# Turning token rows for routing and experts: from TensorE transposes to transposing DMAs, with the tile numbers dealt anew

## The chip, the cores and the metric

The kernel runs on one core of one Trainium2 chip, in float32. The metric is the device time of one execution in microseconds. Instructions run on five engines: TensorE (PE, matrix products and transposes; its weight loads are listed as PEld), VectorE (DVE), ScalarE (ACT), GpSimd (POOL) and SyncE (SP, which here only issues DMAs). A DMA can be issued from the queue of SP, ACT or POOL (in the profile SPq, ACTq, POOLq). Each engine works its own instructions in order and waits where one of them needs something that isn't there yet.

## What is computed

`x` has 3327 rows of 256 numbers, `adj` is a 0/1 matrix of 3327 x 3327. Two layers follow each other:

```python
x = x + gat0(layernorm(x), adj)       # 2 heads of 128; softmax over the neighbours
x = x + moe(layernorm(x))             # 16 experts, 2 for each token
x = x + gat1(layernorm(x), adj)       # 1 head of 256, elu
x = x + recurrent_ffn(layernorm(x))   # 30 steps

# moe
logits = h @ gate_w + gate_b
top_probs, top_idx = top_k(softmax(logits), 2); top_probs /= sum(top_probs)
y = sum over the two experts e of top_prob * ((silu(h @ w1[e]) * (h @ w2[e])) @ w3[e])
```

Here `w1` and `w2` of an expert are 256 x 512 and `w3` is 512 x 256, 1.5 MB together. The change touches only the mixture of experts (`moe`) and what leads up to it.

## The kernel before

**Tiles.** The tokens are padded to 3328 = 26 tiles of 128 (`NP`, `NT`). The span has these stages: first projection (to 53 us), first attention (53 to 388), experts (388 to 752, with the wait for the results' landing at its end), second projection (to 788), second attention (to 1088), recurrence (to 1839).

**First attention (`attend`).** Destination rows are taken in five groups `groups0` of 4, 6, 6, 6 and 4 tiles, each for two heads: ten parts. In each part a loop over `j` runs through the 26 source tiles: ACT makes `e` (L276), DVE masks it to `pT` (L281), PE adds up one product for each destination tile (L286; 1352 products of two passes each in this attention, counted from its start). Between the steps, from `j = 2` on, one piece of other work is let in: first the pieces of `closing` (division by the softmax sum and the residual, then, after the second head, the routing of the rows that are now final: the generator `route`), then those of `later` (the token lists, and the search for the tiles). One `yield` in `route` is thus one step of `j` later in the program. The adjacency comes group by group: GpSimd brings bytes into `in_bytes` (L325), SP turns them into `adjT` by transposing DMAs (L335), one for each tile, 425 KB each. What a group needs is asked for when the lists of an earlier group have been issued. `put_factors` and `row_factors` (L227, L234) spread the row factors, partly over SP.

**Routing (`route`, for one group).** The rows are normalized into `row` (`normalized`: DVE statistics, a power on GpSimd at L121, DVE at L128), stored as float32 in the table `table_x` in DRAM (L516, ACT's queue), and turned on PE two tiles at a time (`turned`, L148; ACT copies the result out of PSUM, L149). The turned rows are the stationary side of the gate products (L526). DVE then finds the two best experts and each token's place in that expert's list, and GpSimd writes token number and weight into `lists` with an indirect DMA for each tile and choice (L592). Group 4 is routed during the first expert tiles, by `aside`.

**Tiles of experts.** `find_tiles` cuts the lists into tiles of 128 tokens of one expert each: 16 from the full tiles of the first three groups (`FIRST`), 45 more when all are routed (61 are `ALWAYS` worked off; further ones only if the data want them). For tile number `s` it gives the expert (`table[0]`), whether its matrices differ from those of tile `s - 3` (`table[1]`), the tokens (`which`), the places of the results (`to`) and the weights. There are `SETS` = 3 sets of matrices; tile `s` uses set `s % 3`, and `weights(s)` loads 1.5 MB on SP (L800 to L802) only where `table[1]` is set.

**Working off (`work_off`).** For tile `s`: GpSimd gathers 128 rows of `table_x` (`gathered`, L761, four tiles ahead), PE turns them by two transposes (`features_first`, L826), ACT copies them to `hT` (L827), PE makes two products of 16 passes each (`product`, L835), ACT the silu (L881), DVE the product of both (L885), PE `results` of the tile before (8 passes, L851), DVE its weighting (L854) and GpSimd scatters it into `given` (L855). In PE's queue a tile is: products of `s`, transposes of `s + 1`, results of `s - 1`.

**Order.** The instruction order within each engine is set by the tile framework's scheduler from this program order, with priorities; the pools (`bufs`) decide what may run ahead. The recurrence already turns its rows by 16-bit planes: ACT parts each float32 into its two 16-bit halves (L1095), SP writes them to DRAM (L1097) and a transposing DMA brings them back with tokens along the free axis (L1107), so that two halves lie beside each other as one float32 again.

Of the kernel before, what the change touches and what calls it, by code (L numbers as in the profile page):

```python
# [31 lines left out]
def gat_moe_gat_recurrent_ffn(ctx: ExitStack, tc: tile.TileContext, a: dict, out: bass.AP):  # L32
# [315 lines left out]
    table_x = dram.tile([NP, D], F32, name="table_x")  # L348
# [33 lines left out]
    with ExitStack() as moe:  # L382
# [125 lines left out]
        turn = moe.enter_context(tc.tile_pool(name="turn", bufs=2))  # L508

        def route(ts):  # L510
# [3 lines left out]
            normalized([x[:, t, :] for t in ts], [row[:, j, :] for j in range(n)])  # L514
            here = slice(t0 * P, (t0 + n) * P)
            nc.scalar.dma_start(table_x[here, :].rearrange("(t p) d -> p t d", p=P), row[:, :n, :])  # L516
            yield

            if ts is not groups0[-1]:
                yield  # L520
            pg = bank()[:, : n * E].rearrange("p (j e) -> p j e", e=E)
            for j0 in range(0, n, 2):
                hT = turned(row[:, j0 : j0 + 2, :], turn, ps)
                for j in range(2):
                    for k in range(KD):
                        nc.tensor.matmul(  # L526
                            pg[:, j0 + j, :], lhsT=hT[:, j, k, :], rhs=gw[:, k, :], start=(k == 0), stop=(k == KD - 1)
                        )
                yield
# [81 lines left out]
            if ts is groups0[3]:  # L611

                for s in range(3):
                    ahead.append(gathered(s))
# [36 lines left out]
        numbers(two[:, 0, :], [[1, SLOTS]], 0, 0)  # L651
# [10 lines left out]
        def find_tiles(end, s0, n):  # L662
# [30 lines left out]
            tile_no = two[:, 0, :n]  # L693
# [61 lines left out]
        places = []  # L755

        def gathered(s):
            if s % 3 == 0 or s == ALWAYS:
                places.append(rows_p.tile([P, MOST * P], F32, name="rb"))
            row = places[-1][:, (s % 3) * D : (s % 3 + 1) * D]  # L760
            nc.gpsimd.indirect_dma_start(  # L761
                out=row, out_offset=None, in_=table_x[: EARLY * P, :] if s < FIRST else table_x,
                in_offset=bass.IndirectOffsetOnAxis(ap=which[:, s : s + 1], axis=0),
            )
            return row
# [56 lines left out]
        def features_first(row):  # L822
            pt = ps_o.tile([P, 512], F32, name="acc0")[:, :D].rearrange("p (k q) -> p k q", k=KD)
            hT = turn.tile([P, 2, KD, P], F32, name="hT")[:, 0]
            for k in range(KD):
                nc.tensor.transpose(pt[:, k, :], row[:, k * P : (k + 1) * P], ident)  # L826
            nc.scalar.copy(hT, pt)  # L827
            return hT

# [13 lines left out]

        ahead = deque()
# [16 lines left out]
        def work_off(s0, s1, aside):  # L861

            hT = features_first(ahead.popleft())
            made = None
            for s in range(s0, s1 + 1):
# [10 lines left out]
                if s < s1:  # L876
                    if s + 4 < s1:
                        ahead.append(gathered(s + 4))
                    pa = product(hT, ew[s % SETS][0])
                    act = edge("e")  # L880
                    nc.scalar.activation(act, pa, AF.Silu)  # L881
                    next(aside, None)
                    pb = product(hT, ew[s % SETS][1])
                    made = edge("pT")
                    nc.vector.tensor_tensor(made, act, pb, ALU.mult)  # L885
                    if s + 1 < s1:
                        hT = features_first(ahead.popleft())
                if s > max(s0, 1):
                    results(s - 1, hidT)
                if s + SETS - 1 < s1:  # L890
# [14 lines left out]
        ahead.append(gathered(3))  # L905
        weights(1)

# [26 lines left out]
        with tc.If(more > ALWAYS - FIRST):  # L934
            ahead.extend(gathered(s) for s in range(ALWAYS, ALWAYS + 4))
            for s in range(ALWAYS, ALWAYS + SETS - 1):
                weights(s)
# [275 lines left out]
```

## Time and profile before

| | us |
|---|---|
| median of the runs | 1838.48 |
| lowest and highest of 3 runs | 1833.5, 1839.01 |
| the profiled execution | 1841.14 |
| its span, first to last instruction | 1839.4 |
| PE busy in the span | 1787.4 |
| DVE, ACT, POOL busy | 1319.1, 1223.9, 888.4 |
| mean granted TensorE clock | 0.995 of full speed |
| expert transposes L826 | 122 of 273 ns |
| routing transposes L148 | 52 of 283 ns |
| their copies out of PSUM, L149 and L827 | 586 and 372 ns each |
| gather L761, mean | 979 ns of POOL, 61 times |
| list entry L592, mean | 1222 ns of POOL, 52 times |

A line of a timeline has the start in microseconds, the length, the engine (a "q" behind it marks a DMA issue: its length is that of the issue, not of the transfer), the source line, the operation, what is written from what, and how many instructions were joined; in square brackets, the idle time of the engine before it and what ended that. A line of groups has the count, then busy time in all, the mean in nanoseconds, and the idle time before. Windows list the busy time of each engine in a stretch, then the granted TensorE clock as a share of full speed, the mean busy share of the 16 DMA engines and what they moved in GB/s. Matmuls are pipelined, so their durations overlap: starts are the better measure.

### The profile page before, as it was taken

Reading aid. Unit: us, or ns where it says so; the run is one execution under the profiler, and the core shown is the slowest. Engines: PE = TensorE matmul, PEld = TensorE weight load, DVE = VectorE, ACT = ScalarE, POOL = GpSimd, SP = SyncE. Lnnn points to the kernel's source line nnn. Section 1 sums busy time; section 2 is a strip of 40 time slices with the busy share of each in tenths; the row PEclk is TensorE's granted clock in tenths of the full one; section 3 lists DMA queues with packets and bytes.
Section 4 is the critical chain, followed back from the end, with each engine's and each line's share of the span. In section 5 each row is a group of like instructions: output and inputs, shape, how many; then the busy total and the mean of one; then the engine's idle time right before and its main releaser. Section 6 shows DMA issues by size and latency. Waiting matters only on the chain.

```text
span 1839.4 us, 32502 instructions
## 1 busy us (share of the span) xinstructions
PE 1787.4 (97%) x10980; PEld 1631.7 (89%) x10980; DVE 1319.1 (72%) x4039; ACT 1223.9 (67%) x1587; POOL 888.4 (48%) x654
## 2 busy tenths in 40 slices
PE   7999999999999999799999999999999999999997
PEld 6999999898999999688888878888888888888886
DVE  6888878853222222657677678999999999999998
ACT  2877667642111111366666579999999999999994
POOL 3010212155333332100111028988898889888984
PEclk9999999999999999899999999999999999999999
DMA  8887360258999886400000036666667666666667
GB/s 178 114 123 91 66 101 16 67 187 255 349 345 333 304 301 225 159 9 22 14 18 22 12 84 172 172 172 168 171 167 178 173 172 172 172 167 169 175 172 218
DMA packets 458610, 284.44 MB, mean 155 GB/s; under 512 B 305269, under 2 KB 418220, under 8 KB 458442
## 3 DMA queue, kind: packets, MB, share of 16 engines
q1 hardware_dynamic: 442322, 249.47, 48.4%
q0 software_dynamic: 11440, 28.09, 8.8%
q10 hardware_dynamic: 4680, 4.76, 0.8%
q8 instruction: 90, 1.47, 0.3%
q14 instruction: 78, 0.64, 0.1%
HBM read 168.19 MB, written 91.69 MB: 141 GB/s over the span
## 4 chain that ended last, share of the span: by engine, by line
PE 67%; issue 10%; DVE 6%; POOL 5%; DMA 3%; ACT 1%; another core or an unknown queue 0%; SPq 0%; POOLq 0%; DVEq 0%; ACTq 0%
PE po L1120 35%; PE acc L286 24%; PE bank L1085 4%; DVE pT L281 3%; POOL given L855 2%; POOL rb L761 2%; DMA given<-wh,to 2%; PE bank L835 1%; PE acc L163 1%; PE bank L148 1%; DMA old<-kept 1%; PE bank L526 1%; PE acc L851 1%; DMA lists<-pair,ati 0%; DVE x L1130 0%
## 5 line engine op out<-in xcount | busy, mean ns | idle before, releaser
L276 ACT ACTIVATE e<-rb,minus,full 128x384 f32<-128x384 f32 (+3 forms) x494 | 399.2, 823 | 168.6 <-DVE pT L281 150.8
L1055 POOL TENSOR_TENSOR th<-th,x 128x1024 f32<-128x1024 f32 (+1 forms) x210 | 465.0, 2214 | 94.1 <-ACT th L1052 86.4
L281 DVE SCALAR_TENSOR_TENSOR pT<-e,part,adjT 128x384 f32<-128x384 f32 (+3 forms) x494 | 383.5, 782 | 117.8 <-PE acc L286 101.9
L1120 PE MATMUL po<-wc,adjT 128*128 128x256 f32 x1888 | 422.2, 379 | 0.0
L1120 PEld LDWEIGHTS po<-wc,adjT 128*128 128x128 f32 x1888 | 356.4, 190 | 47.6 <-DVE x L1130 0.3
L1130 DVE SCALAR_TENSOR_TENSOR x<-po,rr,bb 128x256 f32<-128x256 f32 x780 | 325.1, 478 | 61.8 <-PE po L1120 61.2
L286 PE MATMUL acc<-wh,pT 128*128 128x129 f32 x2704 | 311.0, 276 | 2.3 <-DVE pT L281 2.3
L286 PEld LDWEIGHTS acc<-wh,pT 128*128 128x128 f32 x2704 | 305.5, 192 | 3.6 <-DVE pT L281 3.0
L286 PE MATMUL acc<-s_wh,pT 128*128 128x257 f32 x1352 | 295.5, 381 | 3.6 <-DVE pT L281 3.6
L286 PEld LDWEIGHTS acc<-s_wh,pT 128*128 128x128 f32 x1352 | 255.8, 190 | 42.7 <-DVE pT L281 7.0
L1120 PE MATMUL po<-wc,zT 128*128 128x256 f32 x1232 | 281.0, 379 | 0.8 <-DVE x L1130 0.8
L1064 DVE BATCH_NORM_STATS2 stats<-z 128x6 f32<-128x256 f32 x780 | 274.1, 412 | 1.4 <-ACT z L1059 1.4
L1120 PEld LDWEIGHTS po<-wc,zT 128*128 128x128 f32 x1232 | 229.2, 190 | 29.7 <-issue 1.1
L1095 ACT COPY adjT<-z 128x1024 int16<-128x1024 int16 x236 | 235.2, 1044 | 4.8 <-DVE pT L281 2.0
L121 POOL TENSOR_TENSOR rstd<-ve,neg_half 128x4 f32<-128x4 f32 (+3 forms) x28 | 32.0, 1141 | 410.4 <-DVE ve L119 312.3
L1052 ACT ACTIVATE th<-x 128x1024 f32<-128x1024 f32 (+1 forms) x210 | 209.2, 996 | 29.0 <-DVE x L1130 23.8
L1075 POOL TENSOR_TENSOR rr<-rr,neg_half 128x4 f32<-128x4 f32 (+1 forms) x210 | 206.8, 985 | 26.4 <-DVE rr L1070 26.3
L1059 ACT ACTIVATE z<-th 128x1024 f32<-128x1024 f32 (+1 forms) x210 | 207.0, 986 | 7.9 <-POOL th L1055 1.8
L885 DVE TENSOR_TENSOR pT<-e,bank 128x512 f32<-128x512 f32 x61 | 41.9, 688 | 179.7 <-PE bank L835 119.6
L881 ACT ACTIVATE e<-bank 128x512 f32<-128x512 f32 x61 | 36.4, 597 | 196.9 <-PE bank L835 117.2
L835 PEld LDWEIGHTS bank<-hT,wh 128*128 128x128 f32 x1280 | 149.6, 192 | 9.3 <-issue 4.5
L835 PE MATMUL bank<-hT,wh 128*128 128x128 f32 x1280 | 150.6, 276 | 6.5 <-ACT hT L827 2.5
(196 smaller groups left out, 1546.6 us busy)
## 6 DMA issues: line engine op xcount, KB each, us to landing
wh<-in_w_dram SPq DMA_DIRECT2D x120, 512.0 KB
apart<-adjT SPq DMA_DIRECT2D x236, 256.0 KB
first_set<-in_w_dram SPq DMA_DIRECT2D x63, 512.0 KB
in_bytes<-in_adj_dram POOLq DMA_DIRECT2D x3, 2496.0 KB
adjT<-apart SPq DMA_TRANSPOSE x236
x<-in_x_dram SPq DMA_DIRECT2D x6, 512.0 KB
kept<-x SPq DMA_DIRECT2D x8, 384.0 KB
old<-kept SPq DMA_DIRECT2D x6, 512.0 KB
```

The costliest lines, as they stand in the source:

```text
L276: nc.scalar.activation(e[:, : n * P], rb[:, : n * P], AF.Relu, scale=sc.full[:, j, h : h + 1], bias=sc.minus[:, j, h : h + 1],)
L281: masked = nc.vector.scalar_tensor_tensor(pT[:, : n * P], e[:, : n * P], sc.part[:, j, h : h + 1], adjT[:, j // 2, ts[0] * P : (ts[-1] + 1 ...
L286: nc.tensor.matmul(po[c], lhsT=pT[:, c * P : (c + 1) * P], rhs=wh[:, j, h, :], start=(j == 0 and c % per_bank == 0), stop=(j == NT - 1), s ...
L835: nc.tensor.matmul(p[:, f, :], lhsT=w[:, k, f * P : (f + 1) * P], rhs=hT[:, k, :], start=(k == 0), stop=(k == KD - 1),)
L1052: self.put(nc.scalar.activation(self.th, self.hs, AF.Tanh, scale=1.0 / S))
L1055: self.put(nc.gpsimd.tensor_tensor(self.th, self.th, self.hs, ALU.add))
L1059: self.put(nc.scalar.activation(self.z, self.th, AF.Silu, scale=1.0 / S))
L1064: self.put(nc.vector.bn_stats(stats[:, j, :], self.z[:, j, :]))
L1075: self.put(nc.gpsimd.tensor_tensor(r, r, neg_half[:, : self.n], ALU.pow))
L1095: self.put(nc.scalar.copy(parts[:, c : c + 2], halves[:, c : c + 2]))
L1120: nc.tensor.matmul(self.po[:, j, :], lhsT=self.zT(j, k), rhs=wc[:, k, :], start=(k == 0), stop=(k == KD - 1),)
L1130: nc.vector.scalar_tensor_tensor(self.hs[:, j, :], self.po[:, j, :], self.r[:, j : j + 1], bb, op0=ALU.mult, op1=ALU.add)
```

## The change

Three things are changed together.

1. `table_x` holds each row as two planes of 16-bit halves (`[NP, 2 * D]` of int16; the same bytes as before, parted). `route` parts the normalized rows with ACT copies, two tiles at a time into one buffer `planes`, writes each pair from ACT's queue, and then brings the whole group back by one transposing DMA on SP, over the buffer `row` itself. The gate products read the turned rows there; the transposes L148 and the copies L149 of the routing are gone. There are more yields: between the pairs, and 7 (4 for the last group) before the gate products, where there was one more (none for the last).
2. Experts: `gathered` brings the planes of 128 rows; `put` writes them to one of six DRAM buffers `asked` (on SP for the first three tiles, then on ACT's queue), and `face` brings them back turned into `hT` by a transposing DMA on SP. `features_first` with its PE transposes and its copy is gone. `turn` has 4 buffers instead of 2.
3. Tile numbers: slot `s` of the first 16, and of the 45 later ones, no longer gets tile number `s`; the numbers are dealt to the three lanes `s % 3` in blocks, so that consecutive slots of one lane (which share a set of matrices) get consecutive tile numbers.

```diff
-    table_x = dram.tile([NP, D], F32, name="table_x")
+    table_x = dram.tile([NP, 2 * D], I16, name="table_x")
...
-        turn = moe.enter_context(tc.tile_pool(name="turn", bufs=2))
+        turn = moe.enter_context(tc.tile_pool(name="turn", bufs=4))
...
             normalized([x[:, t, :] for t in ts], [row[:, j, :] for j in range(n)])
+            yield
+            halves = row.bitcast(I16).rearrange("p j (d b) -> p j b d", b=2)
+            for j in range(0, n, 2):
+                planes = gate.tile([P, 2, 2, D], I16, name="planes")
+                nc.scalar.copy(planes, halves[:, j : j + 2])
+                here = slice((t0 + j) * P, (t0 + j + 2) * P)
+                nc.scalar.dma_start(
+                    table_x[here, :].rearrange("(t p) c -> p t c", p=P), planes.rearrange("p j b d -> p j (b d)")
+                )
+                if j + 2 < n and ts is not groups0[-1]:
+                    yield
             here = slice(t0 * P, (t0 + n) * P)
-            nc.scalar.dma_start(table_x[here, :].rearrange("(t p) d -> p t d", p=P), row[:, :n, :])
-            yield
-
-            if ts is not groups0[-1]:
+            turned_rows = row.rearrange("p j d -> p (j d)")[:, : KD * n * P]
+            turned_rows = turned_rows.rearrange("p (k q) -> p k q", k=KD)
+            nc.sync.dma_start(
+                row.rearrange("p j d -> p (j d)").bitcast(I16)[:, : KD * n * 2 * P].rearrange("p (k q) -> p k q", k=KD),
+                table_x[here, :].rearrange("t (b d) -> (t b) d", b=2), transpose=True,
+            )
+            for _ in range(7 if ts is not groups0[-1] else 4):
                 yield
             pg = bank()[:, : n * E].rearrange("p (j e) -> p j e", e=E)
             for j0 in range(0, n, 2):
-                hT = turned(row[:, j0 : j0 + 2, :], turn, ps)
-                for j in range(2):
+                for j in range(j0, j0 + 2):
                     for k in range(KD):
                         nc.tensor.matmul(
-                            pg[:, j0 + j, :], lhsT=hT[:, j, k, :], rhs=gw[:, k, :], start=(k == 0), stop=(k == KD - 1)
+                            pg[:, j, :], lhsT=turned_rows[:, k, j * P : (j + 1) * P], rhs=gw[:, k, :],
+                            start=(k == 0), stop=(k == KD - 1),
                         )
                 yield
...
-        numbers(two[:, 0, :], [[1, SLOTS]], 0, 0)
+        for s0, n in ((0, FIRST), (FIRST, ALWAYS - FIRST)):
+            no = 0
+            for lane in range(SETS):
+                here = two[:, 0, s0 + lane : s0 + n : SETS]
+                numbers(here, [[1, here.shape[1]]], no, 0)
+                no += here.shape[1]
+        numbers(two[:, 0, ALWAYS:], [[1, SLOTS - ALWAYS]], ALWAYS - FIRST, 0)
...
         def gathered(s):
             if s % 3 == 0 or s == ALWAYS:
                 places.append(rows_p.tile([P, MOST * P], F32, name="rb"))
-            row = places[-1][:, (s % 3) * D : (s % 3 + 1) * D]
+            rows = places[-1].bitcast(I16)[:, (s % 3) * 2 * D : (s % 3 + 1) * 2 * D]
...
+        def put(queue):
+            put_down.append(next(asked))
+            queue.dma_start(put_down[-1], ahead.popleft())
+
+        def face():
+            hT = turn.tile([P, KD, P], F32, name="hT")
+            nc.sync.dma_start(
+                hT.bitcast(I16), put_down.popleft().rearrange("t (b d) -> (t b) d", b=2), transpose=True
+            )
+            facing.append(hT)
...
-        def features_first(row):
-            pt = ps_o.tile([P, 512], F32, name="acc0")[:, :D].rearrange("p (k q) -> p k q", k=KD)
-            hT = turn.tile([P, 2, KD, P], F32, name="hT")[:, 0]
-            for k in range(KD):
-                nc.tensor.transpose(pt[:, k, :], row[:, k * P : (k + 1) * P], ident)
-            nc.scalar.copy(hT, pt)
-            return hT
...
         def work_off(s0, s1, aside):
-            hT = features_first(ahead.popleft())
+            hT = facing.popleft()
...
                     nc.scalar.activation(act, pa, AF.Silu)
+                    if s + 3 < s1:
+                        put(nc.scalar)
                     next(aside, None)
...
                     if s + 1 < s1:
-                        hT = features_first(ahead.popleft())
+                        hT = facing.popleft()
                 if s > max(s0, 1):
                     results(s - 1, hidT)
+                next(aside, None)
+                if s + 2 < s1:
+                    face()
                 if s + SETS - 1 < s1:
                     weights(s + SETS - 1)
                 next(aside, None)
...
-        ahead.append(gathered(3))
+        gathered(3)
+        for _ in range(3):
+            put(nc.sync)
+        face()
         weights(1)
+        face()
```

More of the change, by code (lines that the diff above doesn't have):

```diff
@@ L613, in route @@
                 for s in range(3):
-                    ahead.append(gathered(s))
+                    gathered(s)
             if ts is groups0[2]:
@@ L692, in find_tiles @@
             yield
-            tile_no = two[:, 0, :n]
+            tile_no = two[:, 0, here]
             mine = room_m[:E, :, :n]
@@ L753, in find_tiles @@
             nc.vector.tensor_tensor(to[:, here], tof, spare, ALU.add)
-        places = []
+        places, asked = [], cycle([dram.tile([P, 2 * D], I16, name=f"asked{q}") for q in range(6)])
+        ahead, put_down, facing = deque(), deque(), deque()
         def gathered(s):
@@ L759, in gathered @@
                 places.append(rows_p.tile([P, MOST * P], F32, name="rb"))
-            row = places[-1][:, (s % 3) * D : (s % 3 + 1) * D]
+            rows = places[-1].bitcast(I16)[:, (s % 3) * 2 * D : (s % 3 + 1) * 2 * D]
             nc.gpsimd.indirect_dma_start(
-                out=row, out_offset=None, in_=table_x[: EARLY * P, :] if s < FIRST else table_x,
+                out=rows, out_offset=None, in_=table_x[: EARLY * P, :] if s < FIRST else table_x,
                 in_offset=bass.IndirectOffsetOnAxis(ap=which[:, s : s + 1], axis=0),
             )
-            return row
+            ahead.append(rows)
+        def put(queue):
[7 more added lines that the diff above has]
+            facing.append(hT)
         behind = None
@@ L842, in edge @@
             return run.tile([P, MOST * P], F32, name=name)[:, :HID].rearrange("p (f q) -> p f q", f=FH)
-        ahead = deque()
         def results(s, hidT):
@@ L877, in work_off @@
                     if s + 4 < s1:
-                        ahead.append(gathered(s + 4))
+                        gathered(s + 4)
                     pa = product(hT, ew[s % SETS][0])
@@ L934, in gat_moe_gat_recurrent_ffn @@
         with tc.If(more > ALWAYS - FIRST):
-            ahead.extend(gathered(s) for s in range(ALWAYS, ALWAYS + 4))
+            for s in range(ALWAYS, ALWAYS + 4):
+                gathered(s)
+            for _ in range(3):
+                put(nc.scalar)
             for s in range(ALWAYS, ALWAYS + SETS - 1):
+                face()
                 weights(s)
```

## The prediction

> **What bounds the kernel now.** I read the engine totals first, then the stage windows, then the timeline of each place that the change touches.
>
> ```profile
> PE 1787.4 (97%) x10980; PEld 1631.7 (89%) x10980; DVE 1319.1 (72%) x4039; ACT 1223.9 (67%) x1587; POOL 888.4 (48%) x654
> ```
>
> TensorE (PE) is busy for 1787.4 of 1839.4 us and runs its queue in order: a pass taken off it is worth its time, and a new wait in its queue costs its length. The windows of the expert stage (columns: length, busy PE, PEld, DVE, ACT, POOL, clock, DMA share, GB/s):
>
> ```profile
> 388.40:404.90 16.50, 13.97 (x102) 13.14 (x102) 6.59 (x24) 2.25 (x5) 8.86 (x9) 0.90 0.95 316
> 404.90:455.60 50.70, 46.72 (x355) 43.77 (x353) 17.11 (x66) 11.07 (x21) 24.82 (x23) 1.00 0.83 268
> 455.60:710.00 254.40, 254.37 (x1942) 245.09 (x1943) 56.16 (x107) 44.25 (x92) 87.88 (x90) 1.00 0.94 320
> ```
>
> From 455.6 us no PE time is lost; the 4 us missing earlier are the waits at 392.7 (2.5), 433.3 (2.3) and 454.0 (1.6), the first beside weight loads. One tile of the steady stretch, PE's timeline:
>
> ```profile
> 543.94 0.38 PE L826 MATMUL acc<-ident,rb 128*128 128x128 f32 x2
> 544.15 1.89 PE L851 MATMUL acc<-first_set,pT 128*128 128x256 f32 x8
> 545.88 3.73 PE L835 MATMUL bank<-hT,wh 128*128 128x128 f32 x32
> 549.45 0.38 PE L826 MATMUL acc<-ident,rb 128*128 128x128 f32 x2
> ```
>
> The period is 549.45 - 543.94 = 5.51 us. From start to start the two transposes take 544.15 - 543.94 = 0.21, with rounding 0.22, though their durations say 0.38: passes overlap, so I price by starts.
>
> **Gains.** (1) Experts: 61 tiles x 0.22 = **-13.4 us**. (2) Routing inside the attention, groups 0 to 3: 22 token tiles x 2 passes x 0.11 (spacing of L148 starts) = **-4.9**; group 4 is routed in the expert stage, 8 passes, **-0.9**. Together **-19.2**. ScalarE loses 13 copies L149 (0.586) and 61 copies L827 (0.372) and gains 13 plane copies. Their like is the copy of 128x1024 int16 of the recurrence, 1.044 us:
>
> ```profile
> L1095 ACT COPY adjT<-z 128x1024 int16<-128x1024 int16 x236 | 235.2, 1044 | 4.8 <-DVE pT L281 2.0
> ```
>
> ScalarE is 67% busy and is late nowhere by these: taken as 0. If it were, the attention would pay at most 9 x 1.044 - 9 x 0.586, some 4 us.
>
> **New waits, group 0 of the routing.** The gate products now wait for a chain: plane copy, write, transposing DMA on SP, landing. SP's timeline where before has the gate:
>
> ```profile
> 117.96 12.77 SPq L335 DMA_TRANSPOSE adjT<-in_bytes  x6
> 130.83 0.49 SPq L227 DMA_DIRECT2D factors<-first_set  x1
> ```
>
> and PE's:
>
> ```profile
> 114.76 0.96 PE L526 MATMUL bank<-gate_w,hT 128*128 128x16 f32 x8
> ```
>
> In the built order of after, group 0's transposing DMA stands on SP behind all 16 adjacency transposes and the factors, so it is issued at about 131.4, whatever the rows were ready at (112 to 114 us, plus two copies and two writes, is some 10 us earlier). Six adjacency transposes took 12.77 us, 2.13 each for 425 KB, so 512 KB want 2.6 us; behind the ones in flight, which land 4.5 to 5.3 us after issue, I take the landing at 136.3. The gate moves back in PE's queue by 7 yields less one, to the 305th product of the attention, at 127.35 in before, 124.6 without the transposes (0.9) and the gate passes (1.8) that stood ahead of it there. PE then waits 136.3 - 124.6 = **+11.7** (8 to 14). A pause this long costs clock as well: in the first window the 2.53 us wait was followed by 8 L851 in 3.18 us instead of 1.89, the granted clock 0.5 for 3.41 us. I add **+1.7**.
>
> [...]
>
> **Groups 1 to 3.** There is one planes buffer, so copy, write, copy, write, copy, write, transpose follow each other, each write landing before the next copy. The nearest rows: write of 256 KB, 2.1 to 2.25 us to landing; copy 1.04; transpose of 768 KB 1.24 of issue and 3.5 to 5.5 to landing. From the normalized rows to turned rows: 3 x (1.05 + 2.2 + 0.6 of issue and wait) + 0.4 + 5.5 = 17.5, up to 20.7 with the adjacency loads beside it; PE comes to the gate some 16.5 us after the rows. +1 to +4 each, more where SP stands in adjacency transposes (group 1): together **+7.5** (0 to 15).
>
> **Start of the experts.** This is the largest doubt. Before (POOL, then ACT and PE):
>
> ```profile
> 388.43 0.97 POOL L592 DMA_INDIRECT lists<-pair,ati  x1 [0.31 <-issue]
> 389.70 0.99 POOL L761 DMA_INDIRECT rb<-table_x,which  x1 [0.30 <-issue]
> ...
> 393.23 1.04 POOL L121 TENSOR_TENSOR rstd<-ve,neg_half 128x4 f32<-128x4 f32 x1
> ```
> ```profile
> 394.35 0.60 ACT L881 ACTIVATE e<-bank 128x512 f32<-128x512 f32 x1 [7.87 <-remote]
> ```
>
> The attention ends at 388.4 (T0). In the built order of after, POOL holds gathers 3 to 8, then the 12 list entries of group 3 (1.28 each with their gap), then gathers 9 to 14, then the rstd of group 4. ScalarE holds, ahead of the first silu, the put of tile 9, which waits for gather 9 behind those lists; behind silu 0 stands group 4's first plane copy, which waits for that rstd, and only then silu 1. In order: the lists of group 3 come 6 steps of j later (24 to 36 products of 0.22, 5 to 8 us) and end at about T0 + 8 to 10 with part of the gathers 3 to 8 ahead of them, gathers 9 to 14 take 6 x 1.28, rstd at T0 + 20 or so. A gather lands 3.05 us after its issue (363.03 to 366.08), so put 9 goes at about T0 + 14, the table load of 1.28 follows, silu 0 comes at **T0 + 17.5** instead of T0 + 6, silu 1 at about T0 + 23. PE can make products 0 (3.6) and 1 (3.5), then waits; two results and three products later it is in step. Lost: about 16.5 us where before loses 4.5 (the 2.5 and the half clock): **+12** (5 to 16). Had silu 0 only the wait of before, this would be 0.
>
> **Steady tiles.** Per tile: one gather (as before), a write of 128 KB from ScalarE's queue and a transposing DMA of 128 KB on SP. The recurrence does 256 KB of both in about 2 us of all 16 DMA engines (0.67 of some 3 us), so 1.0 a tile; the loads of matrices (1.5 MB; 4.9 us at 320 GB/s) fall from 57 tiles to 30, worked out from the inputs: 27 loads gone pay for it twice over. PE wants the face three tiles after its put; write and transpose land in 2.2 and 3.1 us, against 16 us. Taken as 0; if the chain were late, 1 us a tile is +40 at most, a tail that I cut. The waits at 433.3 and 454 are on loads and mostly go: **-2** (-4 to +4).
>
> [...]
>
> Nothing after 752 us is changed.
>
> **Sum.** -19.2 + 11.7 + 1.7 + 7.5 + 12 - 2 = +11.7. The profiled execution took 1841.1, so 1852.8; the median of the runs shown is 1838.5, 2.6 below it, so **1850 us**.
>
> **Rivals.** (a) *About the same:* the start of the experts costs only its lower bound 5, and the routing 12: -19.2 + 15.0 = -4 to 0, about 1836. Chance 0.18. (b) *Faster:* the routing's chain is hidden. Its place is SP's queue: if the transposing DMA of group 0 lands before PE is at the 305th product (124.6), PE doesn't wait there, nor, with the same chain a little longer against the same cover, in groups 1 to 3; the 20.9 us of routing waits go and the start of the experts stays: -19.2 + 12 - 2 = -9, **1829.5**. Against it: the 16th adjacency transpose was issued at about 128.5, and the release at 117.96 is the landing of an adjacency load, which the change doesn't touch. [...] Chance 0.16. (c) *Much slower:* tiles wait in the steady stretch, or group 0 ends at 140 and silu 0 at T0 + 22: -19.2 + 33 + 7, **1860** and more. For it: the DMA share of 0.94; against it the 27 loads saved. Chance 0.16. (d) *The dealt numbers do not save the loads* (each set still gets a new expert): a tile then needs 0.94 x 5.51 + 1.0 = 6.2 us of DMA, +0.67 over its period where I counted -0.22, over 61 tiles +41 in place of -13.4: about 1905. Chance 0.02; the numbers worked out from the inputs speak against it. The forecast keeps 0.48.
>
> **Range:** all unknowns at their low ends together lie 20 under the sum (3.7 + 7.5 + 7 + 2), at their high ends 20 above it (2.3 + 7.5 + 4 + 6), that is 1830 to 1870; as they are not likely to fall all one way, I take off 2 and 4: 1832 to 1866, which leaves out (b), (d) and the end of (c). A difference under 0.3% (5.5 us) cannot be told from none: faster 0.17 (b and the low edge), same 0.19 (a), slower 0.64.
>
> **What would show it.** Right: no L826 on PE; period of 5.29; PE idle of 8 to 14 us before the gate products of group 0, released by a DMA; a first silu 15 us or more after the last L286; DMA share of the stage near 0.6. Wrong: the gate of group 0 without a wait, silu 0 within T0 + 8, idle PE between tiles after 460 us. If gains hold but one wait is missing, its term was mis-sized.

## The result, and the profile after

The changed kernel takes **1925.53 us** (median of 6 runs, 1921.08 to 1930.43) against 1837.04 of the kernel before on the same chip (6 runs, 1833.5 to 1839.01): a ratio of 1.0484, with a 95% interval of 1.0464 to 1.0504. It is slower, as forecast, but by 88 us instead of 12, and outside the range. The profiled execution took 1921.08 us, its span is 1919.4 us, the mean granted clock 0.979 (before: 0.995).

The engine totals answer to the first line shown of before:

```profile
PE 1801.9 (94%) x10806; PEld 1629.5 (85%) x10806; DVE 1323.1 (69%) x4039; ACT 1204.3 (63%) x1526; POOL 883.7 (46%) x660
```

TensorE has 174 instructions less in its records and is busy 14.5 us longer, part of it work at half the clock: eight gate products of group 0 took 1.86 us there against 0.96 before. Its idle time grew from 52 to 117.5 us. Two things went wrong at once, waits and clock. The windows (columns: length, busy PE, PEld, DVE, ACT, POOL, clock, DMA share, GB/s) say where:

```profile
0.00:414.80 414.80, 375.76 (x3054) 367.81 (x3055) 315.67 (x731) 262.58 (x316) 76.84 (x93) 0.95 0.58 97
414.80:433.40 18.60, 5.46 (x47) 5.11 (x46) 3.44 (x18) 1.25 (x1) 14.51 (x15) 0.80 0.91 205
433.40:500.00 66.60, 56.62 (x387) 52.99 (x388) 20.87 (x78) 10.64 (x16) 22.72 (x21) 0.88 0.81 217
500.00:812.00 312.00, 283.99 (x2045) 257.91 (x2044) 58.24 (x111) 30.57 (x52) 90.99 (x94) 1.00 0.68 189
```

The first is all up to the end of the attention, the second the start of the experts, the third the tiles beside the routing of group 4 and the second search, the last the steady stretch. In before PE lost nothing in the steady stretch at a DMA share of 0.94; here it loses 28 us at 0.68, and every wait of 0.3 us and more in it ends with DVE's product L909, none with a DMA. So the lost time there is not DMA time.

**Balance.** The span grew by 80.0 us. The attention ends at 414.84 instead of 388.44: **+26.4**. From there to the last result pass (L873, at 815.22; before 740.32) it takes 400.4 instead of 351.9: **+48.5**. From there to the second attention -0.7; second attention and recurrence, whose code is unchanged, +5.8.

**Group 0 of the routing.** The timelines of SP and PE:

```profile
118.84 12.55 SPq L335 DMA_TRANSPOSE adjT<-in_bytes  x6
...
132.17 2.18 SPq L529 DMA_TRANSPOSE row<-table_x  x1
```
```profile
137.00 1.86 PE L539 MATMUL bank<-gate_w,row 128*128 128x16 f32 x8 [10.45 <-DMA row<-table_x]
```

The transposing DMA is issued behind the last six adjacency transposes, PE waits 10.45 us for it, and the gate products that follow take twice their time (1.86 against 0.96): the clock is at half for 17.07 us from 129.05.

**Start of the experts.** POOL, then ACT, then PE:

```profile
425.00 0.99 POOL L782 DMA_INDIRECT rb<-table_x,which  x1 [0.30 <-issue]
...
432.27 1.04 POOL L121 TENSOR_TENSOR rstd<-ve,neg_half 128x4 f32<-128x4 f32 x1
```
```profile
410.71 21.36 ACTq L790 DMA_DIRECT2D asked<-rb  x3
432.15 1.28 ACT L903 ACT_TABLE_LOAD   x1 [20.70 <-DMA rb<-table_x,which]
```
```profile
434.82 3.78 PE L873 MATMUL acc<-first_set,pT 128*128 128x256 f32 x8 [12.83 <-DVE pT L909]
```

On POOL the gathers 9 to 14 begin at 425.00, behind twelve list entries (408.7 to 424.7). The first ACT line joins three puts: those of tiles 7 and 8 go at once, that of tile 9 stands from 411.6 to 431.7 until gather 9 has landed, 6.7 us after its issue. The first silu, which needs no gather, stands behind it: it comes at 433.45, 18.6 us after the end of the attention. PE has made one product and part of the next, then waits 12.83 us.

**Second search.** DVE and PE:

```profile
483.44 0.48 DVE L876 TENSOR_SCALAR wh<-acc,weight 128x256 f32<-128x256 f32 x1 [11.64 <-DMA given<-wh,to]
```
```profile
484.93 1.49 PE L732 MATMUL bank<-bb,vec 16*128 16x51 f32 x6 [8.49 <-DVE bb L716]
```

The weighting L876 writes one of two places, and waits until the scatter of the tile two before has read it; that scatter stands on POOL behind eight list entries (465.61 to 478.7). The search's DVE steps stand behind L876, and PE's L732 waits for them. The waits of before in this stretch, at 433.3 and 454.0, were 2.3 and 1.6 us.

**Steady tiles.** PE's timeline over two tiles, which answers to the one shown of before:

```profile
600.01 1.56 PE L873 MATMUL acc<-wh,pT 128*128 128x256 f32 x6 [0.85 <-DVE pT L909]
601.41 3.73 PE L859 MATMUL bank<-hT,wh 128*128 128x128 f32 x32
604.98 0.60 PE L873 MATMUL acc<-wh,pT 128*128 128x256 f32 x2
606.35 1.56 PE L873 MATMUL acc<-wh,pT 128*128 128x256 f32 x6 [0.77 <-DVE pT L909]
```

The transposes are gone, as written. But the order has turned over. Before, PE made the products of tile `s`, the transposes of `s + 1` and then the results of tile `s - 1`, whose inputs had long been there. Now, behind the products of a tile (x32, to 604.98) and the rest of the tile before (x2), come six of the eight result instructions of the **same** tile. They need its silu (0.60) and its product (0.69) first, so PE waits, 0.41 to 0.85 us in each tile. For the tile above, DVE's product is this line; it ends at 606.30, and the six start at 606.35:

```profile
605.61 0.69 DVE L909 TENSOR_TENSOR pT<-e,bank 128x512 f32<-128x512 f32 x1 [5.65 <-PE acc L873]
```

Four tiles (575.65 to 600.01) take 24.36 us: a period of 6.09, against 5.51 before and the 5.29 forecast. The waits are 0.53 of the 0.8 on average; the rest is that the eight results, parted in two, take 1.40 + 0.60 us of PE, where eight in a row take 1.73 (604.14 - 602.41 in the first experiment).

### The profile page after: what moved, and what is told of

Read it like the earlier page. It is cut to its first block, busy times and chain, and to the rows that moved or that the text cites. A ratio compares the mean times of both kernels' runs of the same rounds, so it can differ in the third digit from the quotient of the medians.

```text
span 1919.4 us, 32260 instructions
## 1 busy us (share of the span) xinstructions
PE 1801.9 (94%) x10806; PEld 1629.5 (85%) x10806; DVE 1323.1 (69%) x4039; ACT 1204.3 (63%) x1526; POOL 883.7 (46%) x660
## 3 DMA queue, kind: packets, MB, share of 16 engines
q8 instruction: 88, 1.44, 0.3%
## 4 chain that ended last, share of the span: by engine, by line
PE 51%; DVE 3%; DMA 3%; issue 3%; POOL 1%; ACT 1%; SPq 0%; ACTq 0%; POOLq 0%; DVEq 0%
PE po L1155 32%; PE acc L286 14%; PE bank L1120 3%; DMA given<-wh,to 2%; PE acc L163 1%; DVE pT L281 1%; DVE x L1165 1%; DMA old<-kept 1%; DVE stats L1099 0%; POOL th L1090 0%; PE bank L148 0%; POOL given L877 0%; DVE x L1173 0%; ACT adjT L1130 0%; DVE low L1039 0%
## 5 line engine op out<-in xcount | busy, mean ns | idle before, releaser
L1090 POOL TENSOR_TENSOR th<-th,x 128x1024 f32<-128x1024 f32 (+1 forms) x210 | 464.9, 2214 | 98.6 <-ACT th L1087 91.9
L281 DVE SCALAR_TENSOR_TENSOR pT<-e,part,adjT 128x384 f32<-128x384 f32 (+3 forms) x494 | 382.7, 782 | 147.6 <-PE acc L286 118.5
L286 PE MATMUL acc<-wh,pT 128*128 128x129 f32 x2704 | 319.6, 281 | 10.4 <-DVE pT L281 10.4
L286 PEld LDWEIGHTS acc<-wh,pT 128*128 128x128 f32 x2704 | 315.1, 197 | 12.2 <-DVE pT L281 12.0
L909 DVE TENSOR_TENSOR pT<-e,bank 128x512 f32<-128x512 f32 x61 | 41.9, 687 | 249.4 <-PE bank L859 230.4
L877 POOL DMA_INDIRECT given<-wh,to x61 | 59.9, 982 | 220.7 <-DVE wh L876 212.5
```

The costliest lines, as they stand in the source:

```text
L281: masked = nc.vector.scalar_tensor_tensor(pT[:, : n * P], e[:, : n * P], sc.part[:, j, h : h + 1], adjT[:, j // 2, ts[0] * P : (ts[-1] + 1 ...
L286: nc.tensor.matmul(po[c], lhsT=pT[:, c * P : (c + 1) * P], rhs=wh[:, j, h, :], start=(j == 0 and c % per_bank == 0), stop=(j == NT - 1), s ...
L1090: self.put(nc.gpsimd.tensor_tensor(self.th, self.th, self.hs, ALU.add))
```

## The experiments

My theory after the comparison: (1) PE's new order costs about 0.8 us a tile; (2) the start of the experts is lost to puts in front of silu on ACT; (3) the attention is lost to the transposing DMAs of the routing, waits and clock. The rivals: the DMA chain (gather, write, transpose) is late in the steady tiles whatever the order; behind the first wait stands another that is just as late; the dealt numbers cost something. Each time of before is from the same chip as the run that it stands beside.

**Results in their old place.** After, with the first result pass of each tile kept where the program has it:

```diff
+                one = nc.tensor.matmul(po, lhsT=hidT[:, f, :], rhs=w3[:, f, :], start=(f == 0), stop=(f == FH - 1))
+                if f == 0 and s > 0:
+                    tc.keep_in_program_order(one)
```

> After, with one edit: the first pass of the results of tile s - 1 is pinned in PE's queue behind the products of tile s, the order of before. Theory 1 (PE's order): after lost its time in the steady tiles because the scheduler put three of four result passes of tile s straight behind the products of tile s, so that PE waits each time for silu and product of ScalarE and VectorE, 0.42 to 0.85 us; the period is 6.09 instead of 5.29. Pinned, the period falls to 5.3, 52 tiles x 0.80 = 42 us: about 1884 us. The attention (its end 415 us) and the late start of the experts stay. Rival (the DMA chain): the faces or the matrices come late and PE would wait for them instead; then the waits change their releaser to a DMA, the period stays near 6.0, and the time near 1925.

1887.84 us against 1836.91, ratio 1.0282 (1.0253 to 1.0312): 38 us of the 88 are gone. PE's timeline:

```profile
602.41 1.89 PE L873 MATMUL acc<-wh,pT 128*128 128x256 f32 x8
604.14 3.73 PE L859 MATMUL bank<-hT,wh 128*128 128x128 f32 x32
607.71 1.89 PE L873 MATMUL acc<-first_set,pT 128*128 128x256 f32 x8
```

All eight result instructions stand together and wait for nothing; the period is 607.71 - 602.41 = 5.30, the forecast one. From 551 to 770 us PE is busy 218.97 of 219 at a DMA share of 0.77. Theory 1 holds, and the rival of late faces falls as the cause of the 6.09: the chain keeps step at 5.30. It is not without waits: four single ones of 0.93 to 1.74 us stand between 511 and 547, two of them for matrices and one for a face (1.19).

**Puts behind their silu as well.** The same, and each put pinned to its place behind the silu on ACT:

```diff
-                        put(nc.scalar)
+                        tc.keep_in_program_order(put(nc.scalar))
```

> As the run with the results pinned, and each put of an expert tile is also pinned on ScalarE's queue behind the silu of the tile that issues it, so that no put waits for a gather ahead of the first silu. Theory 2 (queue order at the start): the first silu comes at T0 + 6 to 8 instead of T0 + 18.5, T0 the end of the attention, and PE loses 3 to 5 us there instead of 16: about 11 less than the run with the results pinned alone, 1873 us. Rival (the faces need the long lead): with puts only three tiles ahead PE waits for faces in the steady stretch, the period rises over 5.3, and the gain at the start is eaten; 1884 or more.

1893.52 us, ratio 1.0313 (1.0283 to 1.0343): 6 slower than the run before it, not faster. Silu 0 does come 2.1 us after the end of the attention. Then POOL, DVE and PE:

```profile
431.06 1.04 POOL L121 TENSOR_TENSOR rstd<-ve,neg_half 128x4 f32<-128x4 f32 x1
```
```profile
432.13 0.73 DVE L128 TENSOR_SCALAR row<-x,mv,rstd 128x256 f32<-128x256 f32 x2 [11.22 <-POOL rstd L121]
```
```profile
433.52 3.78 PE L873 MATMUL acc<-first_set,pT 128*128 128x256 f32 x8 [9.16 <-DVE pT L911]
```

The power `rstd` of group 4 stands on POOL behind twelve list entries (411 to 427) and three gathers; DVE waits for it, and the product that PE needs (L911) stands behind it on DVE. Theory 2 in its simple form fell: the put was the first of two waits with the same source, GpSimd's list entries, and taking it away uncovered the second. Steady waits of about 3 us (at 542.8, 574 and 605) came on top, the first two for matrices; the profile names nothing for the third.

**The gate of the routing on TensorE again.** After, with the transposes and copies of the routing put back; the planes are still written to the table, and PE's new order in the experts is left in:

```diff
-            nc.sync.dma_start(
-                row.rearrange("p j d -> p (j d)").bitcast(I16)[...], table_x[here, :]..., transpose=True,
-            )
-            for _ in range(7 if ts is not groups0[-1] else 4):
-                yield
+                        nc.tensor.transpose(pt[:, j, k, :], row[:, j0 + j, k * P : (k + 1) * P], ident)
+                    nc.scalar.copy(hTs[j], pt[:, j])
```

> After, with the turning of the rows for the gate products given back to PE (transposes and copies as before, no transposing DMA in the routing, no extra yields ahead of the gate); the planes are still copied and written for the experts, the experts are as in after. Theory 3: the waits for turned rows, the clock after them and the later lists cost the attention 26 us net; it ends at 389 to 392 instead of 415 and the whole takes about 1925 - 25 = 1900 us. Rival: the attention is late because ScalarE has the plane copies or the DMA engines have the extra writes; then it ends at 400 or later and the time stays above 1910.

1908.0 us, ratio 1.0392 (1.0362 to 1.0422), 17 less than after where 25 were expected. Up to the 1144th product of the attention it is 3.2 us behind before (335.1 against 331.9), where after is 19.4 behind: theory 3 holds for groups 0 to 2. But the attention ends at 405.83, because the puts now stand among the last `e` of the attention. ACT and PE:

```profile
390.30 1.52 ACT L276 ACTIVATE e<-rb,minus,full 128x512 f32<-128x512 f32 x2 [6.57 <-DMA rb<-table_x,which]
```
```profile
391.95 11.48 PE L286 MATMUL acc<-wh,pT 128*128 128x129 f32 x88 [4.57 <-DVE pT L281]
```

ACT waits 6.57 us for a gather (the put's input) before it may make the next `e`: the wait moved from the experts into the attention.

**The dealt numbers alone.** The kernel before, with only part 3 of the change.

> Before, with only the tile numbers dealt anew: 30 loads of matrices instead of 57. PE has no waits for matrices from 456 us on in before, so theory: 0 to -4 us (the waits at 433 and 454 may go), 1833 to 1838 us, DMA share of the expert stage down from 0.94 to about 0.6. Rival (the dealing itself costs, for example by a longer search or a slower start): over 1843.

1836.44 us, ratio 0.9998 (0.9987 to 1.001). The steady stretch, from 500 to 700 us:

```profile
500.00:700.00 200.00, 200.00 (x1527) 192.57 (x1526) 43.84 (x80) 35.49 (x73) 70.26 (x72) 1.00 0.48 151
```

The DMA share there falls from 0.94 to 0.48, and the time doesn't move: the loads were hidden before. Dealing is worth nothing by itself and costs nothing.

**The gates later.** The results in their old place, and more steps between the transposing DMA and the gate:

```diff
-            for _ in range(7 if ts is not groups0[-1] else 4):
+            for _ in range((17, 9, 9, 7, 4)[groups0.index(ts)]):
```

> As the run with the results pinned (1887.8 us), and the gate products of groups 0 to 3 are moved back further, by 17, 9, 9 and 7 yields instead of 7, so that the turned rows of groups 0 to 2 have landed when PE comes to them. Theory (waits and the clock behind them): PE's waits of 10.6 + 1.7 us at group 0, about 2 us each at groups 1 and 2, and the half clock behind each (126.2 to 146.7, 228.6 to 235.4, 310.5 to 317.3) go: 16 us of waits and about 11 of clock, less 1 to 3 for lists that come later; about 1862 to 1866 us. Rival (the waits cost only themselves, and half clock costs little beside other work): 1871 or more. Rival 2 (later lists push the start of the experts back by as much as is won): 1880 or more.

1892.65 us (1885.72 and 1899.58; the profile is of the slower) against 1842.04, ratio 1.0278 (1.0232 to 1.0323). The wait and the half clock of group 0 do go: product 436 of the attention comes at 157.3, in the first experiment at 173.4, 16.1 earlier. Then it is given back, first in group 1 (ACT, then PE):

```profile
202.06 1.95 ACT L276 ACTIVATE e<-rb,minus,full 128x768 f32<-128x768 f32 x2 [7.88 <-DMA adjT<-in_bytes]
```
```profile
204.20 4.48 PE L286 MATMUL acc<-wh,pT 128*128 128x129 f32 x24 [4.53 <-DVE pT L281]
```

ACT's write of planes (issued at 201.64, ahead of this `e`) came only when an adjacency transpose had landed, whose data it doesn't need: in the trace it signals on the same semaphore as the transpose that SP issued at 196.85, and waits for that one's end at 201.56. In after the write at 123.47 waits for the transpose issued at 118.84 in the same way: both name semaphore 108, which the transpose raises for the last time at 123.40, and ACT's wait for it ends at 123.43. In that trace all DMA issues of SP and ACT name eight semaphores between them, 101 to 108. At the end of the attention PE then waits 1.07, 3.88, 2.18 and 9.20 us between 409 and 430, beside GpSimd's unbroken lists and gathers (405 to 427.9), and the attention ends at 432.09. Theory 3 is right on the place and the price (16 us for group 0), wrong in that moving the gate would save it: all that is put off there meets the end of the attention.

**The gate on TensorE, everything pinned.** Results and the puts of the first eight tiles kept in place, the gate on TensorE, the planes parted and written only behind the gate.

> All remedies on one kernel: gate products turned on PE at the place that they have in before, plane copies moved behind them, experts fed by gather, put and face with the results pinned behind the next tile's products and the first puts pinned behind their silu, tile numbers dealt. Theory: the attention ends as in before (388 us, up to +3 for 13 plane copies on ScalarE), the expert tiles take 5.30 instead of 5.51 us, -13 in all, and the start costs what it costs in before, +0 to +5: 1824 to 1832 us, under before. Rival (the transposing DMAs cost PE more than 0.22 us a tile in waits, wherever they stand): 1837 or more.

1882.23 us, ratio 1.0228 (1.021 to 1.0246), not the 1824 to 1832 expected. Up to the 1257th product it is 6 us behind before (373.1 against 367.1), then it stalls (374 to 388) and ends at 405.68; the experts take 363.4, with a wait of 6.13 us for the gate of group 4, whose copy stood on ACT behind a plane copy that waited 5.53 for a write.

**And gathers 3 to 8 behind the lists on GpSimd.** The same with these gathers and the plane copies pinned as well (`tc.keep_in_program_order`).

> As the run with the gate on PE and all pins (1882 us), and the gathers of tiles 3 to 8 are pinned on GpSimd behind the list entries of group 3, the plane copies on ScalarE behind what was traced before them. In that run the masking on VectorE (L281) stood up to 3 us at a time from 374 to 388 us while GpSimd issued lists and gathers without a pause, though the records of its inputs had ended; group 4's gate waited 6 us for a copy that stood behind a plane copy. Theory (GpSimd's unbroken indirect DMAs hold VectorE up): the attention ends at 389 to 394 instead of 406, group 4's gate waits under 1 us, the tiles keep 5.30; in all 1850 to 1860 us. Rival (the stall comes from the puts and faces of tiles 0 to 2 that stand in the same stretch, or from something else): the attention still ends after 400 and the time stays above 1868.

1874.78 us against 1841.96, ratio 1.017 (1.0153 to 1.0187); the best of those whose table holds planes. The wait for group 4's gate is gone, the stall at the end of the attention is not. DVE and PE:

```profile
382.28 0.75 DVE L281 SCALAR_TENSOR_TENSOR pT<-e,part,adjT 128x512 f32<-128x512 f32 x1 [4.01 <-remote]
```
```profile
383.08 7.11 PE L286 MATMUL acc<-wh,pT 128*128 128x129 f32 x42 [3.93 <-DVE pT L281]
```

By the records of ACT and PE, what they hand to this L281 was there before 379.2; "remote" names no releaser. So gathers 3 to 8 ahead of the lists are not its cause. The trace narrows it: the semaphore that PE raises for this L281 was raised at 382.19, 382.28 and 382.37, while the last ends in PE's records are 375.42, 376.66 and 379.15. Before 371 and after 383 the two lie 0.02 us apart (ends of matrix products are modelled). In the two other runs with such stalls, too, signals of PE come where its records have no end. So DVE waits for PE's signal and isn't itself held. Why the signal is late **stays open**. The rival's numbers came (end after 400, time over 1868), but puts and faces of tiles 0 to 2 aren't it alone: they stand beside the last steps of the attention in after too (386.4 to 390.7), and DVE doesn't stall there. Nor are GpSimd's list entries alone: in before, twelve of them run from 369.7 to 389.4 beside the same L281, and there it is they that are longer (seven take 1.48, the last two 0.97) while PE waits for nothing over 0.34 us. What lengthens them is not shown: four entries of 0.95 us in before, from 229.19 to 237.23, ran beside L281 as well.

**Only the later tiles turned by DMAs.** The kernel before with dealt numbers, routing, table and the first 16 tiles untouched; for tiles 16 to 60 ACT parts the gathered rows, writes them, and SP brings them back turned. The results stay in their place.

```diff
+        def put():
+            planes = turn.tile([P, 2, KD, P], F32, name="hT").rearrange("p a k q -> p (a k q)").bitcast(I16)
+            planes = planes[:, : 2 * D].rearrange("p (b d) -> p b d", b=2)
+            nc.scalar.copy(planes, ahead.popleft().bitcast(I16).rearrange("p (d b) -> p b d", b=2))
...
+                    if s0 == 0 and FIRST <= s + 3 < s1:
+                        put()
...
-                        hT = features_first(ahead.popleft())
+                        hT = features_first(ahead.popleft()) if s + 1 < FIRST or s0 > 0 else facing.popleft()
```

> The kernel before (routing on TensorE, float32 table, tile numbers dealt anew) with only the 45 later tiles turned by transposing DMAs: ScalarE parts the gathered rows into planes, writes them, SP brings them back turned; the first pass of the results of those tiles keeps its place behind the products of the next tile. Theory (the loss sits in the routing, in the start of the experts and in the order on TensorE, and the passes saved in the steady tiles are worth their time): period 5.51 up to tile 15, 5.29 to 5.30 after it, 45 x 0.22 = 9.9 less: 1827 us, ratio 0.9946, DMA share in the steady stretch about 0.8. Rival (the chain of copy, write and transpose or SP's queue makes steady tiles late, as with the waits for loads seen with the routing on TensorE): waits of 1 to 3 us at single tiles, 1835 to 1850.

1839.88 us (12 runs) against 1835.49 (17 runs), ratio 1.0025 (1.0016 to 1.0035). The period behind the switch is 5.30 (starts of L874 at 545.36, 550.70, 556.00), so 45 x 0.21 are saved; PE loses them again in new waits: 1.50, 1.39, 1.05, 1.94 and 1.64 us between 491 and 520, 0.74 at 608 and 1.11 at 641, together 9.4. Five of the seven end with a load of matrices, as the first does, and none with a face:

```profile
491.64 2.02 PE L858 MATMUL bank<-face,wh 128*128 128x128 f32 x16 [1.50 <-DMA wh<-in_w_dram]
```

The theory fell, and what the rival foretold came; why loads that are on time with the dealing alone are late here is not shown. The median lies 4 us above the profiled execution (1835.92), so most runs lose still more.

**The same without dealing.**

> The same with the tile numbers as they were before. Theory (all DMAs share the 16 engines, and the share before leaves no room): a tile took 0.94 x 5.51 = 5.18 us of DMA before; write and transpose add 0.77 x 5.30 - 0.48 x 5.51 = 1.44 by the two runs that have the dealt numbers with and without them; together 6.6 against 5.29, so 45 tiles are late by 1.3 each: about 1885 us, share 0.95 or more, waits for matrices and faces. Rival (the share counts waiting as well, and the transfers fit in beside each other): no more than 10 us above the run with the dealt numbers.

1878.85 us, ratio 1.0218 (1.0197 to 1.024). The window from 540 to 740 us, first of the run with the dealt numbers, then without:

```profile
540.00:740.00 200.00, 195.22 (x1458) 186.23 (x1457) 43.51 (x75) 37.67 (x65) 61.48 (x63) 1.00 0.71 188
```
```profile
540.00:740.00 200.00, 176.43 (x1264) 161.23 (x1263) 35.35 (x64) 34.29 (x62) 55.78 (x58) 0.99 1.07 313
```

The DMA share is 1.07, and a tile takes 6.40 us (eight tiles from 565.56 to 616.75), near the 6.6 worked out by adding shares; PE's waits there end with loads of matrices. The transfers do come on top of each other, and without the dealt numbers DMA would bound the stage; with them it doesn't.

**From tile 24 on.** As the run from tile 16 on, with `FIRST + 8` for `FIRST`.

> As the run with only the later tiles turned by DMAs, with the dealt numbers, but from tile 24 on instead of 16: at tiles 16 to 22 TensorE had lost 7.5 us in five waits, where ScalarE's queue holds six loads of parameters (issues from 479.1 to 485.6, between the puts) and GpSimd's gathers wait for the copies. Theory (those waits come from the neighbours at the switch, not from the chain of copy, write and transpose): they go; 37 x 0.22 = 8.1 less than the kernel before, 1 to 2 lost in single waits for loads: 1829 to 1831, ratio 0.996 to 0.997. Rival (any switch from one way to the other costs such waits, since put and face of the first tiles come late against the loads of matrices): 1834 to 1840.

1842.57 us (11 runs) against 1840.94 (15 runs), ratio 1.0003 (0.9994 to 1.0012). The waits at 491 to 520 are gone, but others come at the new switch. POOL, ACT and PE:

```profile
551.73 0.94 POOL L767 DMA_INDIRECT rb<-table_x,which  x1 [4.84 <-ACT hT L842]
```
```profile
555.40 0.62 ACT L842 COPY hT<-rb 128x512 int16<-128x512 int16 x1 [1.90 <-DMA asked<-hT]
...
555.92 1.08 ACT L906 ACTIVATE e<-bank 128x512 f32<-128x512 f32 x2
```
```profile
557.29 3.78 PE L874 MATMUL acc<-wh,pT 128*128 128x256 f32 x8 [4.38 <-issue]
```

A gather waits until ACT has copied an older row out of the buffer (three tiles share one); ACT's copies wait, by the profile, until earlier writes (`asked<-hT`) have landed; the silu stands behind such a copy; PE waits 4.38 us, and the clock is at half for 6.83 us from 556.55. This profiled execution took 1847.0, the slowest of its runs; whether the others have this wait is not shown. No version was faster than the kernel before.

## Why the prediction was wrong

The forecast added 11.7 us to the span; 80.0 came. Step by step:

- **"Steady tiles ... Taken as 0", and the gain "61 tiles x 0.22": the step that failed.** The passes saved are real: 5.30 with the results in their place. But I took PE's order of before and struck out two passes, though the scheduler builds the order anew; it put the results of a tile directly behind that tile's own products. The transposes had been what kept silu and product covered. 5.29 forecast, 6.09 measured: over the stage some 41 us of miss, and 38 came back when only the order was restored. The new order stood in the built kernel, before any run. Why the scheduler chose so is not settled. My question there, whether the face comes in time, was the wrong one: it did. The tail "+40 at most", which the sum left out, has the size that came only by luck: it was for a late chain.
- **Routing waits, "+11.7" and "+7.5".** All PE waits of 0.3 us and more in the attention came to 25.1 us against 5.4 before: +19.7 for 19.2 forecast, but the sum is right partly by luck. The waits named, for turned rows, are 10.45 at group 0 and 1.26, 2.09 and 1.04 at groups 1 to 3: 14.8 us, each in its range. The chain behind them was not sized right in each part: the transposes of 768 KB took 3.13 to 3.77 us to issue and landed 5.25 to 6.67 us after their start, and the 1.24 put down for their issue is about what one of 256 KB took in before (1.25 at 1198.80). Another 10.2, against 2.1 before, are for DVE's `pT`, which I had not foreseen; the copies and writes on ScalarE were "taken as 0". Two examples: the 1.92 at 126.1 goes back to ACT's write that waits for an adjacency transpose, the 1.77 at 210.1 to the normalization, which stands ahead of the masking on DVE and waits for GpSimd:

```profile
207.13 2.03 DVE L128 TENSOR_SCALAR row<-x,mv,rstd 128x256 f32<-128x256 f32 x6 [1.25 <-POOL rstd L121]
```
```profile
210.14 10.99 PE L286 MATMUL acc<-wh,pT 128*128 128x129 f32 x96 [1.77 <-DVE pT L281]
```

- **Clock, "I add +1.7": mis-sized.** 26.4 - 19.7 + 4.9 (transposes gone) leaves 11.6 us. The clock records show half speed for 17.07, 3.41, 3.41, 6.83 and 6.83 us in the attention, of which PE worked some 28: up to 14 us lost, which covers it. I priced one record of 3.41 for one wait. Waits of 1 to 3 us (227.8, 307.3, 365.6, 387.0) each had one beside them as well; those of 1.77 and 1.76 at 210.1 and 289.6 had none.
- **Start of the experts, "+12".** Silu 0 at 18.6 us after the attention instead of 17.5; waits of 1.73 and 12.83 and about 2.4 of clock, 17 us against 4.2 before: +12.8. Right, by the chain named; gather 9 took 6.7 us to land, where I took 3.05. I had not seen that a second wait of 9 us lies under it.
- **"The waits at 433.3 and 454 ... -2": wrong.** They became +7.4 (8.49 of wait and about 3 of clock, against 4.0 before): the second search moved to a place where scatters stand behind eight list entries. I had asked whose loads those waits were on, not what else was queued on POOL. With the dealing alone waits of 1.98 and 0.67 stay near there (442.8 and 451.9). The three waits that I listed ahead of 455.6 add up to 6.4 us, not 4; no term rests on that.
- **DMA.** I priced write and transpose at 1.0 us a tile. By shares it is 0.77 x 5.30 - 0.48 x 5.51 = 1.44. That it fits in came from the dealt numbers, as forecast; rival (d) has the right mechanism, shown by the run without dealing (6.40 measured, 6.2 forecast), but the numbers do save the loads.
- **Rivals.** (a) and (b) are out: no wait was hidden. (c), "1860 and more", is what came, at a chance of 0.16: it named tiles that wait in the steady stretch as one of its ways, and priced it at 7. Of my signs, no L826, the wait of group 0 and the late silu came; the period of 5.29 did not, and idle PE between tiles, a sign of "wrong", did.
- **Not foreseen.** +5.8 us in second attention and recurrence, whose code is the same. In after 5.0 of it lies in one stretch near 1750 us. There a short DVE instruction, L1105, stands four times for about 2 us, always from a start inside GpSimd's L1090 to just behind that one's end:

```profile
1731.02 2.38 POOL L1090 TENSOR_TENSOR th<-th,x 128x1024 f32<-128x1024 f32 x1
1731.30 2.12 DVE L1105 TENSOR_SCALAR rr<-v 128x4 f32<-128x4 f32 x1
```

Begun outside of such an instruction, it takes at most 0.24 us. In before the same pair starts the other way round, DVE first by 0.06 us (1655.25 and 1655.31), and DVE is done in 0.17. In these two stages five of the six other runs whose table holds planes have 4.5 to 6.5 more than before, and 18 to 28 of their 210 L1105 begin inside such an L1090 (in after 17); the sixth has 1.3 more, and the runs built on the kernel before -1.1 to +0.1, with 2 or 3 each (before: 2). By these ends it is DVE that stands there, until GpSimd's instruction is through; what ties the two, and why they meet in these runs, stays open.

Together the misses are 41.7 (order), 9.4 (search), 10.4 (attention: waits 0.5, the rest, which the clock covers, 9.9), 0.8 (start), 5.8 and -0.7, and 0.9 in the expert stage that I can't place: 68.3, which is 80.0 - 11.7.

The half clock in the attention of after comes in lengths that are all multiples of 3.41 us, and in before and after it also starts at whole multiples of 3.41 us from one start to the next (in after 30 and 23 of them between 129.05, 231.45 and 309.95). Short waits had it behind them too: 0.91 and 1.26 us of idle time, up to 222.0 and 227.8, came ahead of 3.41 us of half clock from 231.4, and 1.04 up to 387.0 ahead of 6.83 from 388.5. Not each had: the two of 1.8 us in the attention of after, those of 2.34 and 1.68 up to 435.6 and 455.6 in before and the five of 1.05 to 1.94 in the run from tile 16 on had no half clock behind them. What decides between the two is not shown.

## What to carry to other kernels

When instructions go from the engine that bounds a loop, read its new order in the built kernel before pricing it: they may have been the cover of a wait, and a scheduler doesn't put the rest back as it was. A DMA that waits for its input on a compute engine's queue can hold up what stands behind it (in after the put of tile 9 stood on ScalarE's queue from 411.6 to 431.7, ahead of the first silu), and where several such waits hang on one busy queue (here GpSimd's list entries), moving one uncovers the next (12.83 us of PE's wait in after, 9.16 with the puts moved). Price the pauses of TensorE with the half clock that can follow: in the attention of after it is put at 11.6 us on 19.7 of new waits, while single waits of 1.7 and 2.3 us in before had none.

## What the runs showed of the hardware

- In the attention of after, half clock of 3.41 or 6.83 us beside some waits of only 1 to 3 us and none beside others; around the wait for group 0's turned rows 17.07 us in after (a wait of 10.45) and 20.48 with the results in their old place (10.6). In before and after its starts lie whole multiples of 3.41 us apart.
- Worked out by shares, 5.18 us a tile for the DMAs of before and 1.44 for write and transpose make 6.62; a tile with both took 6.40 us at a share of 1.07. At 1.07 of share the 16 engines moved 313 GB/s, at 0.94 some 320.
- A DVE instruction of 0.17 us (L1105, 128x4) that began inside a GpSimd instruction of 1.3 to 2.4 us (L1090) ended 0.02 to 0.18 us behind it, 17 times in after and twice in before (there L1070 and L1055).
- In before seven list entries on GpSimd from 374.65 to 385.37 took 1.48 us beside DVE's L281, the next two 0.97; four beside L281 from 229.19 to 237.23 took 0.95. Waits of 2 to 10.5 us of DVE's L281 at the end of the attention, in three runs, end with a late signal of PE that stays unexplained.
